# A causal attention layer: VectorE's maximum issued ahead of ScalarE's copy, and inverse roots as exp(-½ ln)

## The chip, the core and the metric

The kernel runs on one core of a Trainium2 chip. A core has five engines with a queue each: TensorE (PE; its weight loads are listed apart as PEld), VectorE (DVE), ScalarE (ACT), GpSimd (POOL) and SyncE (SP, which here starts DMAs). Every engine takes its own instructions strictly in order, and the engines wait for each other by semaphores. The metric is device time in microseconds (us), the median over runs.

## The reference, cut to what matters

Three stages run one after the other on a 64 x 64 image of 256 channels, which is 4096 tokens of 256 values: a windowed linear attention, a causal softmax attention with a small two-layer network behind it, and a mixture of experts. The change lies in the second:

```python
def _layernorm(x, g, b):
    mu = jnp.mean(x, axis=-1, keepdims=True)
    var = jnp.var(x, axis=-1, keepdims=True)
    return (x - mu) * jax.lax.rsqrt(var + LN_EPS) * g + b      # LN_EPS = 1e-5
...
A = jnp.einsum('bqd,bkd->bqk', q, k)
A = jnp.where(causal, A, MASK_FILL) / sqrt(D)
out = jnp.einsum('bqk,bkd->bqd', softmax(A), v) + x
out = _layernorm(out, g_ln, beta_ln)
h = relu(out @ W1.T + b1) @ W2.T + b2
return _layernorm(h, g_lnff, beta_lnff)      # t = t + this; then t is normalised again for the experts
```

So each group of 512 tokens needs three inverse standard deviations per token: one after the attention, one after the small network, and one for the experts' input.

## The kernel before, in words

All products are float32. The causal stage works on pairs `h` of query tiles (256 queries) and pairs `b` of key tiles (256 keys), with `b` from `h` down to 0. A block (h, b) goes through these steps:

- **scores** (L1160): four matmuls (L1170) write 256 keys x 256 queries into one PSUM bank `pa` of which there are two. ScalarE copies the bank to SBUF as `s` (L1182), and VectorE takes the running maximum over key blocks from the same bank (L1186). At b = 0 VectorE folds the maximum (L1189).
- **maxima** (L1192): TensorE turns the folded maximum (L1199), VectorE reduces it over the keys (L1201, L1205), TensorE turns it back (L1212), ScalarE copies it as `tops` (L1214).
- **exponentials** (L1218): VectorE subtracts `tops` from `s` (L1221), ScalarE takes the exponential (L1222).
- **products** (L1228): matmuls with the values accumulate in `po` (L1243); at b = 0 `finish` (L1250) divides, adds the residual and takes mean and variance (L1258 to L1264).

Up to 19 blocks are scored ahead of their exponentials. When four (at the end two, one, one) query tiles of a group are finished, `layers` (L1271) puts a list of small steps on a line; the main loop takes one step from a line when it is due, in between the scores and products:

- `root(mvs)` (L1278, ScalarE: square root of the variance plus eps), `first` (reciprocal on VectorE, L1281, then the scaling, L1287), `turn` (transposes L1295, ScalarE's `aT` L1296), two times `hidden` (L1304, L1306), `last` for each tile (L1313, L1315 and statistics);
- `root(mvy)`, then `scale` for each tile (L1281 again, L1323, L1324, statistics);
- `root(mine)`, then `norm` (L1281, L1332), and `turn_again` (L1349 and ScalarE's L1353), whose result is the experts' input.

There are ten such lines, so thirty roots. After the last block the rest of the lines is emptied one step after another; then the experts' routing starts, with a softmax (`every` L1342, product L1520, exponential L1493, one-hot columns L1572, L1577) from which the weights to load are found.

The order on TensorE, VectorE and ScalarE is the order in which the program emits (a hand-written schedule); GpSimd's and the DMA queues' follow from a scheduler. Two engines that read the same PSUM bank are put one after the other by semaphores: in the kernel before, the maximum waits for the copy, and the matmuls that take the bank again wait for the maximum. [...]

## Time and profile before

| | |
|---|---|
| time, median of 3 runs (lowest, highest) | 1732.9 us (1732.24, 1734.23) |
| time of the profiled execution | 1732.45 us |
| its span, from the first to the last instruction | 1730.8 us |
| causal stage, from L1027's first products to the experts' L1577 | about 825 to 1501 us |
| PE busy / DVE busy / ACT busy / POOL busy | 96% / 58% / 46% / 31% of the span |
| mean granted TensorE clock | 0.985 |
| ACT table loads at L1222 and at L1278 | 21 and 21, 1283 ns each |

The profile is one execution. A group line reads: source line, engine, operation, output tile <- input tiles, shapes, count, then busy time and the mean of one, then the idle time of that engine just ahead of these instructions, with what ended it. A line of the waits reads: who waited, for whom: us in total, times, the longest. A line of the timeline reads: start, duration, engine, line, operation, tiles, count, and in brackets the idle time ahead of it. PEclk is the TensorE clock that was granted, 1.00 being full speed.

### The profile page before, as it was taken

The page shows a single profiled execution, that of the slowest core. Times are in us where ns is not written, and L with a number is a line of the kernel's source. Part 1 is how long each engine was busy: PE and PEld are TensorE (multiplying, and loading weights), DVE is VectorE, ACT ScalarE, POOL GpSimd, SP SyncE. Part 2 cuts the span into 40 slices and gives each one's busy share as a digit, 9 for nine tenths or more (in the row PEclk, how much of TensorE's full clock was granted, in tenths as well). Part 3 has the DMA queues.
Part 4 walks back from the last instruction along what each step waited for, and adds up shares of the span by engine and source line. Part 5 has one row for each costly group of instructions (what it writes and reads, how often), then busy time and mean ns, then how long its engine had stood idle before and what let it go on. Part 6 is the DMA issues. An engine that isn't in the chain of part 4 may idle for free.

```text
span 1730.8 us, 48947 instructions
## 1 busy us (share of the span) xinstructions
PE 1654.3 (96%) x21131; PEld 1257.4 (73%) x21131; DVE 997.1 (58%) x2101; ACT 793.4 (46%) x1539; POOL 540.8 (31%) x819
## 2 busy tenths in 40 slices
PE   5999999999999999999999999999999998699997
PEld 3666666666766666666778888787787776488996
DVE  6545666566645677676443456555645555655656
ACT  3566444444566445544133344444454444344442
POOL 2485435431381533341300220211112021322322
PEclk9999999999999999999999999999999998799999
DMA  8511312112421312122000000000000000100001
GB/s 251 153 66 64 89 54 69 41 47 64 144 76 52 98 43 55 50 57 77 1 1 1 1 1 0 1 0 1 1 1 1 1 1 1 49 1 25 25 13 37
DMA packets 89768, 74.15 MB, mean 43 GB/s; under 512 B 39568, under 2 KB 73512, under 8 KB 89552
## 3 DMA queue, kind: packets, MB, share of 16 engines
q1 hardware_dynamic: 87136, 63.00, 12.2%
q0 software_dynamic: 1264, 3.84, 0.7%
q10 hardware_dynamic: 1152, 4.19, 0.7%
q8 instruction: 165, 2.70, 0.7%
q14 instruction: 51, 0.42, 0.1%
HBM read 53.18 MB, written 17.83 MB: 41 GB/s over the span
## 4 chain that ended last, share of the span: by engine, by line
PE 41%; DVE 6%; ACT 3%; issue 1%; POOL 0%; ACTq 0%; DVEq 0%; POOLq 0%
PE pa L1170 11%; PE po L1243 11%; PE py L1668 6%; PE rb L1603 4%; PE pm L1099 2%; PE pm L1304 2%; PE cd L1603 1%; PE pm L1313 1%; DVE lnst L863 1%; DVE max L1186 1%; PE pm L1027 1%; ACT s L1182 1%; DVE s L1221 1%; DVE t L1324 1%; PE po L1246 1%
## 5 line engine op out<-in xcount | busy, mean ns | idle before, releaser
L382 ACT ACTIVATE pm<-ps 128x448 f32<-128x448 f32 (+22 forms) x674 | 323.5, 545 | 289.0 <-PE ps L433 156.1
L384 DVE TENSOR_SCALAR pm<-ps 128x448 f32<-128x448 f32 (+13 forms) x406 | 240.6, 621 | 214.0 <-PE ps L433 142.8
L433 PE MATMUL ps<-q,kh 32*128 32x188 f32 (+15 forms) x4224 | 193.9, 330 | 1.9 <-issue 1.7
L1170 PE MATMUL pa<-qT,k 128*128 128x256 f32 (+1 forms) x800 | 185.3, 376 | 0.0
L1186 DVE TENSOR_TENSOR max<-max,pa 128x512 f32<-128x512 f32 x105 | 71.8, 683 | 189.9 <-ACT s L1182 189.8
L1170 PEld LDWEIGHTS pa<-qT,k 128*128 128x128 f32 x800 | 150.6, 191 | 23.8 <-issue 2.7
L1222 ACT ACTIVATE s<-s 128x512 f32<-128x512 f32 x136 | 85.5, 630 | 178.4 <-DVE s L1221 174.7
L466 PE MATMUL ps<-pm,vh 128*32 128x188 f32 (+9 forms) x2688 | 148.2, 336 | 0.0
L433 PEld LDWEIGHTS ps<-q,kh 32*128 32x128 f32 (+1 forms) x4224 | 138.7, 169 | 8.5 <-issue 6.1
L502 POOL TENSOR_TENSOR y<-y,rn 128x512 f32<-128x512 f32 x32 | 40.9, 1278 | 305.5 <-DVE y L501 277.7
L1182 ACT COPY s<-pa 128x512 f32<-128x512 f32 x120 | 69.9, 582 | 115.1 <-PE pa L1170 115.0
L1668 PE MATMUL py<-w,hT 128*128 128x256 f32 x512 | 115.7, 379 | 1.1 <-DVE y L1671 1.1
L466 PEld LDWEIGHTS ps<-pm,vh 128*32 128x32 f32 x2688 | 70.8, 109 | 53.0 <-issue 35.2
L1243 PE MATMUL po<-kh,s 128*128 128x257 f32 x406 | 105.6, 388 | 3.0 <-ACT s L1222 3.0
L1668 PEld LDWEIGHTS py<-w,hT 128*128 128x128 f32 x512 | 97.5, 191 | 14.3 <-DVE y L1671 1.5
L420 PE MATMUL ps<-table,table 32*128 32x256 bf16 (+19 forms) x2752 | 105.5, 251 | 0.2 <-ACT kp L667 0.2
L420 PEld LDWEIGHTS <-table 32*128 32x128 bf16 (+1 forms) x2752 | 40.7, 94 | 85.4 <-issue 83.4
L1221 DVE TENSOR_TENSOR s<-s,tops 128x512 f32<-128x512 f32 x136 | 95.2, 703 | 1.0 <-ACT tops L1214 1.0
L586 PE MATMUL ps<-l0wo,y 128*128 128x256 f32 x384 | 90.7, 387 | 0.0
L1235 POOL TENSOR_SCALAR xn<-t,stats 128x256 f32<-128x256 f32 x32 | 42.0, 1318 | 151.0 <-DVE att L1260 150.6
L1243 PE MATMUL po<-v,s 128*128 128x257 f32 x342 | 87.2, 386 | 1.8 <-ACT s L1222 1.8
L1243 PEld LDWEIGHTS po<-kh,s 128*128 128x128 f32 x406 | 75.9, 194 | 16.4 <-ACT s L1222 4.4
(376 smaller groups left out, 3023.3 us busy)
## 6 DMA issues: line engine op xcount, KB each, us to landing
rn<-rscratch SPq DMA_DIRECT2D x48, 256.0 KB
oscratch<-ov SPq DMA_DIRECT2D x32, 256.0 KB
ov<-oscratch SPq DMA_DIRECT2D x32, 256.0 KB
vq<-vscratch SPq DMA_DIRECT2D x80, 64.0 KB
t<-in_xT SPq DMA_DIRECT2D x16, 256.0 KB
vscratch<-v SPq DMA_DIRECT2D x32, 128.0 KB
vh<-vscratch SPq DMA_DIRECT2D x16, 256.0 KB
out<-y SPq DMA_DIRECT2D x7, 512.0 KB
```

The source lines that it names most:

```text
L382: nc.scalar.activation(dst, src, AF.Relu)
L384: nc.vector.tensor_scalar_max(dst, src, 0.0)
L420: nc.tensor.matmul(got[h][ps, spot].rearrange("p (y x) -> p y x", y=part.r1 - part.r0), lhsT=spread[hs, kind, ks], rhs=bias[hs], start=(i ...
L433: nc.tensor.matmul(got[h][ps, spot].rearrange("p (y x) -> p y x", y=part.r1 - part.r0), lhsT=keys[hs], rhs=q[hs, part.r0 : part.r1, part.c ...
L466: nc.tensor.matmul(out, lhsT=v, rhs=pm[:, h, spot].rearrange("p (y x) -> p y x", y=part.r1 - part.r0), start=fresh, stop=(left[key] == 0), ...
L586: nc.tensor.matmul(pt[:, i * D : (i + 1) * D], lhsT=ys[wi, Y][:, (2 * j + i) * P : (2 * j + i + 1) * P], rhs=wo[:, n, :], start=(n == 0), ...
L1170: nc.tensor.matmul(pp[:, k * 2 * P + at : (k + 1) * 2 * P], lhsT=key, rhs=qT[:, c, q0 + at : q0 + 2 * P], start=(c == 0), stop=(c == DC - 1))
L1182: nc.scalar.copy(s, pp)
L1186: nc.vector.tensor_tensor(u["max"], old, pp, op=ALU.max)
L1221: nc.vector.tensor_tensor(s, s, u["top"].unsqueeze(1).to_broadcast([P, 2, 2 * P]), op=ALU.subtract)
L1243: nc.tensor.matmul(acc, lhsT=u[b][:, (2 * k + j) * P : (2 * k + j + 1) * P], rhs=v[2 * b + k][:, 0 : D + 1], start=(b == h and k == 0), st ...
L1668: nc.tensor.matmul(py, lhsT=hT[:, e, f, j * P : (j + 1) * P], rhs=w2v[:, e, f, :], start=(n == 0), stop=(n == len(order) - 1))
```

## The change

In `scores` the two readers of the bank change places: VectorE's maximum is issued first and waits for the matmuls, ScalarE's copy is issued second and waits for the maximum, and the matmuls that reuse the bank wait for the copy. In `layers` each root becomes two activations on ScalarE, a logarithm with bias eps and an exponential with scale -0.5, so that the inverse root comes from ScalarE; the thirty reciprocals on VectorE go.

```diff
             else:
-                nc.scalar.copy(s, pp)
                 old = u["max"]
                 if b == h - 1:
                     u["max"] = sm.tile([P, 512], F32, name="max", bufs=1)
                 nc.vector.tensor_tensor(u["max"], old, pp, op=ALU.max)
+                nc.scalar.copy(s, pp)
...
             def root(var):
-                nc.scalar.activation(var[:, j0:j1, 1], var[:, j0:j1, 1], AF.Sqrt, bias=eps5)
-
-            def inverse(var):
-                nc.vector.reciprocal(var[:, j0:j1, 1], var[:, j0:j1, 1])
+                nc.scalar.activation(var[:, j0:j1, 1], var[:, j0:j1, 1], AF.Ln, bias=eps5)
+                nc.scalar.activation(var[:, j0:j1, 1], var[:, j0:j1, 1], AF.Exp, scale=-0.5)
 
             def first():
-                inverse(mvs)
...
             def scale(j):
                 mvy = state["mvy"]
-                if j == j0:
-                    inverse(mvy)
...
             def norm():
-                inverse(mine)
```

## The prediction

> **What bounds the kernel now.** I read the page first: which engine is full, and where it is not.

> ```profile
> PE 1654.3 (96%) x21131; PEld 1257.4 (73%) x21131; DVE 997.1 (58%) x2101; ACT 793.4 (46%) x1539; POOL 540.8 (31%) x819
> PE   5999999999999999999999999999999998699997
> ACT  3566444444566445544133344444454444344442
> ```

> TensorE is the bound; only its stops count. The causal stage is slices 20 to 35 (825 to 1501 us), and the only real hole is at its end. So I took the table of stretches and TensorE's waits of the stage's steady part.

> ```profile
> 825.00:1445.00 620.00, 600.99 (x2740) 495.75 (x2741) 321.71 (x725) 260.89 (x457) 108.77 (x186) 0.99 0.00 1
> 1467.00:1490.00 23.00, 16.41 (x77) 12.74 (x75) 19.18 (x61) 9.69 (x32) 2.89 (x4) 0.89 0.00 1
> ...
> PE pm L1199 <- DVE fold L1189: 4.4, 9, 1.7
> PE pm L1304 <- ACT aT L1296: 2.8, 1, 2.8
> PE pm L1212 <- DVE wide L1205: 2.6, 3, 1.9
> PE po L1243 <- ACT s L1222: 2.5, 2, 1.8
> PE pm L1295 <- DVE att L1287: 2.3, 1, 2.3
> PE pm L1349 <- DVE att L1332: 2.0, 1, 2.0
> ```

> The columns of the stretches are the length, then busy time of PE, PEld, DVE, ACT, POOL, then the clock. In 620 us TensorE stops for 19.0 us: all that the steady part can give back, besides clock. In the stage's tail (1467 to 1490) TensorE is no bound; a chain of small steps through VectorE, TensorE and ScalarE runs, and ScalarE is busy for 9.69 of 23 us. The timeline of ScalarE shows why so little:

> ```profile
> 1456.41 0.63 ACT L1222 ACTIVATE s<-s 128x512 f32<-128x512 f32 x1
> 1457.06 1.28 ACT L1278 ACT_TABLE_LOAD   x1
> 1458.36 0.30 ACT L1278 ACTIVATE mvy<-mvy,eps 128x4 f32<-128x4 f32 x1
> 1458.67 1.28 ACT L1222 ACT_TABLE_LOAD   x1
> ...
> 1467.16 1.28 ACT L1278 ACT_TABLE_LOAD   x1
> 1468.46 0.29 ACT L1278 ACTIVATE mvs<-mvs,eps 128x1 f32<-128x1 f32 x1
> ...
> 1489.83 0.29 ACT L1278 ACTIVATE stats<-stats,eps 128x1 f32<-128x1 f32 x1 [1.89 <-DVE stats L864]
> ...
> 1492.69 1.28 ACT L1493 ACT_TABLE_LOAD   x1
> ```

> A root among exponentials costs two loads; but after 1467.16 no exponential comes, and nine square roots (1468.46 to 1489.83) share one load.

> **Loads.** The order of instructions of the built programs can be compared. For the kernel before it has 21 loads at L1278, 21 at L1222 and one at L1493, and the trace has the same numbers, so I trust it for the changed one: a load ahead of each of the 30 logarithms, another ahead of each of the 30 new exponentials, one at L1222, none at the softmax; 61 for 43. Up to 1445 us there are 19 roots, so 39 loads for 37: no change there. The other 16 more fall into the tail.
> [...]

> **The tail.** A new root is load, logarithm, load, exponential. From the rows: 1.28 + 0.02 + 0.30 + 0.01 + 1.28 + 0.02, and the exponential itself, which the trace does not show for 4 columns: between 0.19 (the shortest ScalarE entry, an accumulator read) and 0.30 (the square root with its bias tile). I take 0.20, as it has no bias tile: 3.11 us. Nine of them are 28.0 us. ScalarE's other work from 1467.0 to 1490.1 is 9.69 - 1.28 - 9 x 0.295 = 5.75 us. Together 33.8 us where 23.0 us pass now: ScalarE becomes the bound of the tail, +10.8. It can't run quite without a stop: the last logarithm waits for statistics that VectorE begins only after the copies' column sums are in (L1357, 0.17; then 0.47 + 0.48 + 0.43 + 0.18 with gaps, 1.9 us in all), less the load that runs meanwhile (1.28): +0.6. Before 1467 two roots stand among the last exponentials, where TensorE stops for 2.1, 1.5 and 1.5 us on ScalarE already; each gets two 0.20 us steps longer at most: +0.4. Off go a reciprocal (0.16) and what is not hidden of the softmax's load (0.1). Tail: 10.8 + 0.6 + 0.4 - 0.3 = **+11.5**. Bounds: if only the last line's three roots were on the path, 3 x (3.11 - 0.30 - 0.17) = +8; if half of ScalarE's 13 us of idle time stayed, +17. The row that is nearest is the full queue, so 11.5.

> **The exchange of copy and maximum.** The bank comes free after the same two reads (0.58 and 0.68), and TensorE never waits for a bank (L1170 has no such wait). What changes is who is held.

> VectorE is freed: its maximum waits 237.2 us for the copy now. The fold is ready 0.58 sooner; the nine waits of L1199 (0.55, 0.18, 0.18, 0.99, 0.24, 1.74, 0.18, 0.18, 0.18) lose up to that each: -2.9. The 1.9 at L1212 follows such a fold: -0.6. Where roots' loads stood ahead of a copy, VectorE waited for all of it: the maximum at 1396.80 waits 2.74 for a copy at 1396.20, behind two loads; the scaling L1332 then starts at 1397.61. Without that it starts after the new exponential, 1392.76 + 3.11 = 1395.9: the 2.0 at L1349 loses 1.7. Likewise at 1346: -1.1. At 1210: the scale steps, from 1200.65, move to the second root's end, 1192.2 + 3.1 + 0.6 + 3.1 = 1199.1: -1.5.

> ScalarE is bound: the copy now waits for the maximum, behind whatever VectorE has queued, and exponentials and `aT` are queued behind the copy. Where VectorE is late, TensorE pays:

> ```profile
> 1034.60 0.57 ACT L1182 COPY s<-pa 128x512 f32<-128x512 f32 x1
> 1035.06 1.45 ACT L1296 ACTIVATE aT<-pm,ik 128x512 f32<-128x512 f32 x2
> ...
> 1036.61 0.66 DVE L1186 TENSOR_TENSOR max<-max,pa 128x512 f32<-128x512 f32 x1
> ...
> 1036.87 1.88 PE L1304 MATMUL pm<-aT,ik 128*128 128x512 f32 x4
> ```

> The maximum of this bank stands behind a string of `finish` (1033.94 to 1036.69), perhaps 0.6 sooner than now. So the copy ends at about 1037.3, the halves of `aT` follow by 1038.6, and L1304, ready at 1036.87, stops for about 1.2. The same pattern stands at 1068.05 (copy, then `aT`, with `scale` steps on VectorE): another 1.2. At 1351 L1349 gets about 1.3, since a root's 3.11 at 1343.28 now precedes copy and `aT`. The two waits on exponentials: 0.7 loses 0.5, 1.8 gains 0.3. Sum of the stops: -2.9 - 0.6 - 1.7 - 1.1 - 1.5 + 1.2 + 1.2 + 1.3 - 0.2 = **-4.3**.

> **Clock.** After the stops of 2.79, 2.25 and 2.03 us (at 1211, 1348 and 1399) the clock row is 0.50 for 3.4 us; eight products that take 1.73 elsewhere take up to 3.4: about 1.7 us each. Stops of 1.92, 1.83 and 1.74 were not followed by this. In the changed kernel I expect two such stretches for three: the 1.83 grows to 2.1, and at 1345 to 1351 two stops (1.1 and 1.3) lie close. **-1.7**.
> [...]

> **Free of charge.** The 30 reciprocals (0.17 each) lie on an engine that is idle for half the stage; 19 exponentials in the steady part add 4 us to a ScalarE that is busy for 261 of 620 us. Two GpSimd instruction pairs (L1235 against L1177 and L1179) change order on an idle queue; SyncE's queue is as before. If GpSimd's cover were gone, it would be one 1.3 us step (L1235) each.

> **Sum.** Profiled execution 1732.45, span 1730.8 (the median of the runs, 1732.9, is 0.45 above): 1732.45 + 11.5 - 4.3 - 1.7 = 1738.0 us. About 0.2% (3.5 us) is what a measurement of this kernel can tell from no change.

> **Rivals.**
> *Freed VectorE wins (not slower).* One mechanism: with the 237 us of waits gone, VectorE runs so far ahead that the copies never wait, and the three new stops don't arise. Stops -8.0, all three clock stretches gone -5.1: -13.1; with a tail of +10.8 that gives 1730. It decides once the steady part gains over 12. For it: VectorE is busy for only 52% of the steady part. Against it: the row at 1036.61, where VectorE is late without waiting for anybody.
> *Bound ScalarE loses more.* If the stop of 1.2 comes in each of the seven four-tile lines, the steady part has 8.4 of new stops in place of 2.4, and one or two clock stretches more than I count: +3 in place of -6; with the tail 1747. Against it: in most lines there is more slack than at 1036.
> *The change does not do what the order shows.* If no table load stood between logarithm and exponential, all loads of the stage would go: the 5.1 us of stops at 1452 to 1461, the load at 1467, and the stops and clock of the steady part (-9 with clock), tail +0: about 1718. Against it: the order, whose counts the trace confirms.

> **How the numbers follow.** Forecast 0.60 (own range 1734 to 1743, from a tail of 10 to 14 and a steady part of -8 to -3.5), freed VectorE 0.20, bound ScalarE 0.18, no loads 0.02. Faster than 1729.4: a third of freed VectorE and no loads, 0.08. Within 0.2%: the rest of freed VectorE (0.14) and the forecast's low end (0.10). Slower: 0.68. The range leaves out the fast end of the second case and the slow end of the third: 1729 to 1747.

> **What would show it.** In the profile after: 30 loads each at the two root lines, 1283 ns; ScalarE all but full from 1467 for about 34 us; L1520 some 12 us further behind the last L1243 than now; maxima waiting for PE, copies for DVE; L1199's waits below 2 us in all; new stops at L1304 behind `aT`. If TensorE's stops up to the last score shrink by over 8 us, or the tail grows by less than 8, the forecast is wrong there.

## The result and the profile after

The changed kernel takes **1737.66 us** in the median of 11 runs (1735.58 to 1741.43), the kernel before 1732.36 (11 runs, 1728.87 to 1734.33, the three of the table above among them). The ratio is 1.0032, with a 95% interval from 1.0022 to 1.0043: slower by 5.3 us, or 0.3%. The profiled execution took 1737.66 too, with a span of 1735.9.

The page of the changed kernel, the lines that answer to those shown of the kernel before:

```profile
PE 1652.6 (95%) x21131; PEld 1256.1 (72%) x21131; DVE 995.7 (57%) x2071; ACT 819.9 (47%) x1587; POOL 541.7 (31%) x819
PE   5999999999999999999999999999999997599997
ACT  3567444444566444544133345445454456544442
```

TensorE's busy time is no longer than before; the hole near slice 34 is deeper, and ScalarE is fuller there. VectorE has the 30 reciprocals less, ScalarE 30 steps and 18 loads more. TensorE's waits in the steady part of the causal stage (825 to 1441 us):

```profile
PE pm L1301 <- ACT aT L1293: 2.5, 3, 1.1
PE po L1243 <- ACT s L1222: 2.5, 2, 2.2
PE pm L1212 <- DVE wide L1205: 1.8, 3, 1.1
PE pm L1343 <- ACT aT L1293: 1.6, 1, 1.6
PE pm L1199 <- DVE fold L1189: 1.4, 2, 1.0
PE pm L1292 <- DVE att L1284: 1.0, 1, 1.0
```

The list has changed sides. The waits for VectorE (`fold`, `wide`, `att`) have shrunk, and nearly half of what is left, 6.6 us on the lines shown, is for ScalarE: for exponentials (2.5 us, as before) and for `aT`, which now stands behind copies that wait for maxima. With the small lines that are not shown the sum is 13.7 us, for 19.0 before. Between the two readers it went as forecast: over the whole program the maximum waits 199.1 us for TensorE and the copy 212.7 us for the maximum, where the maximum waited 237.2 us for the copy.

The tail in ScalarE's timeline (start, duration, instruction, idle time ahead of it):

```profile
1464.24 0.81 ACT L1293 ACTIVATE aT<-pm,ik 128x128 f32<-128x128 f32 x2 [2.64 <-PE pm L1292]
1465.06 1.28 ACT L1278 ACT_TABLE_LOAD   x1
1466.36 0.30 ACT L1278 ACTIVATE stats<-stats,eps 128x4 f32<-128x4 f32 x1
1466.67 1.28 ACT L1279 ACT_TABLE_LOAD   x1
1467.97 0.21 ACT L1279 ACTIVATE stats<-stats 128x4 f32<-128x4 f32 x1
...
1477.31 0.81 ACT L1293 ACTIVATE aT<-pm,ik 128x128 f32<-128x128 f32 x2 [1.22 <-PE pm L1292]
...
1494.46 0.29 ACT L1278 ACTIVATE stats<-stats,eps 128x1 f32<-128x1 f32 x1 [0.53 <-DVE stats L864]
1496.07 0.20 ACT L1279 ACTIVATE stats<-stats 128x1 f32<-128x1 f32 x1
```

Load, logarithm, load, exponential, and the next load at 1468.19: from 1464.24 the queue is full but for short stops, with loads as its bulk: 16 of 1283 ns up to the last root's end at 1496.27, 20.5 of 32.0 us. TensorE waits:

```profile
1443.91 1.14 PE L1243 MATMUL po<-vh,s 128*128 128x257 f32 x4 [2.05 <-ACT s L1222]
...
1496.77 1.01 PE L1334 MATMUL pm<-ik,att 128*128 128x1 f32 x4 [6.59 <-DVE att L1326]
...
1506.86 2.02 PE L1571 MATMUL py<-byexpert,b 8*128 8x2 f32 x8 [0.64 <-DVE byexpert L1568]
```

The first and the last of these lines are the marks by which I compare all kernels. In the kernel before they are:

```profile
1452.94 1.14 PE L1243 MATMUL po<-vh,s 128*128 128x257 f32 x4 [2.11 <-ACT s L1222]
...
1501.08 2.02 PE L1577 MATMUL py<-byexpert,b 8*128 8x2 f32 x8 [0.64 <-DVE byexpert L1574]
```

The first is TensorE's stop on the last pair's exponentials: the end of the steady part. The last is the end of the routing, after which the expert stage runs. Their distance is the tail: 62.95 us, for 48.14. The steady part runs from the stage's first matmul at L1099 (846.59 us, before 846.80) to the first mark. It is 8.8 us shorter, the tail 14.8 longer.

### The profile page after: what moved, and what is told of

It reads as the page before. It is cut to its first block, busy times and chain, and to the rows that moved or that the text cites. A ratio compares the mean times of both kernels' runs of the same rounds, so it can differ in the third digit from the quotient of the medians.

```text
span 1735.9 us, 48897 instructions
## 1 busy us (share of the span) xinstructions
PE 1652.6 (95%) x21131; PEld 1256.1 (72%) x21131; DVE 995.7 (57%) x2071; ACT 819.9 (47%) x1587; POOL 541.7 (31%) x819
## 4 chain that ended last, share of the span: by engine, by line
PE 40%; DVE 5%; ACT 5%; issue 1%; POOL 0%; DVEq 0%; ACTq 0%; POOLq 0%
PE pa L1170 11%; PE po L1243 10%; PE py L1662 6%; PE rb L1597 4%; PE pm L1099 2%; PE cd L1597 1%; PE pm L1301 1%; PE pm L1310 1%; ACT L1279 1%; ACT L1278 1%; DVE lnst L863 1%; PE pm L1027 1%; PE po L1246 1%; DVE t L1319 1%; DVE max L1185 1%
## 5 line engine op out<-in xcount | busy, mean ns | idle before, releaser
L1170 PE MATMUL pa<-qT,k 128*128 128x256 f32 (+1 forms) x800 | 184.5, 375 | 0.0
L1186 ACT COPY s<-pa 128x512 f32<-128x512 f32 x120 | 70.1, 584 | 212.7 <-DVE max L1185 212.7
L1170 PEld LDWEIGHTS pa<-qT,k 128*128 128x128 f32 x800 | 149.6, 190 | 23.3 <-issue 2.2
L1222 ACT ACTIVATE s<-s 128x512 f32<-128x512 f32 x136 | 85.3, 629 | 70.8 <-DVE s L1221 70.4
L1243 PE MATMUL po<-kh,s 128*128 128x257 f32 x406 | 105.6, 388 | 3.0 <-ACT s L1222 3.0
L1235 POOL TENSOR_SCALAR xn<-t,stats 128x256 f32<-128x256 f32 x32 | 43.5, 1366 | 157.8 <-DVE att L1260 157.4
L1243 PEld LDWEIGHTS po<-kh,s 128*128 128x128 f32 x406 | 75.8, 194 | 16.4 <-ACT s L1222 4.4
L1243 PE MATMUL po<-v,s 128*128 128x257 f32 x342 | 85.5, 380 | 2.2 <-ACT s L1222 2.2
```

The source lines that it names most:

```text
L1170: nc.tensor.matmul(pp[:, k * 2 * P + at : (k + 1) * 2 * P], lhsT=key, rhs=qT[:, c, q0 + at : q0 + 2 * P], start=(c == 0), stop=(c == DC - 1))
L1243: nc.tensor.matmul(acc, lhsT=u[b][:, (2 * k + j) * P : (2 * k + j + 1) * P], rhs=v[2 * b + k][:, 0 : D + 1], start=(b == h and k == 0), st ...
```

## The experiments

Six kernels, beside the two, by these marks; "stops" are TensorE's recorded stops within the steady part, without the one at the mark, "half clock" its stretches of 3.4 us at half clock (6.8 counts as two). The median is over all runs of a kernel, the other columns are of its one profiled execution. What lies behind the last mark took 229.0 to 232.1 us in these executions, so steady part and tail don't add up to the differences of the medians.

| kernel | median us | loads in the stage | steady us | stops us | half clock | tail us |
|---|---|---|---|---|---|---|
| before | 1732.4 | 43 | 606.1 | 18.3 | 3 | 48.1 |
| changed | 1737.7 | 61 | 597.3 | 13.0 | 1 | 62.9 |
| exchange alone | 1720.9 | 43 | 593.0 | 10.3 | 1 | 48.9 |
| roots alone | 1757.6 | 61 | 616.1 | 22.4 | 6 | 63.1 |
| changed, one shared load | 1708.3 | 1 | 586.3 | 7.2 | 0 | 40.5 |
| changed, square roots in the tail | 1722.9 | 45 | 595.6 | 13.0 | 0 | 48.0 |
| one shared load, copy first | 1714.2 | 1 | 594.6 | 10.5 | 1 | 42.1 |
| changed, aT and hT by VectorE in the tail | 1736.1 | 61 | 599.0 | 13.0 | 2 | 58.8 |

**The exchange alone.** Kernel before, with

```diff
-                nc.scalar.copy(s, pp)
...
                 nc.vector.tensor_tensor(u["max"], old, pp, op=ALU.max)
+                nc.scalar.copy(s, pp)
```

> The kernel before with the exchange of maximum and copy alone; square root and reciprocal stay. Theory (the two parts add: the exchange earns the 9.0 us by which the first stop on an exponential at the end comes earlier, 1452.94 to 1443.91, and the roots' loads cost the 14.8 us by which the tail is longer): TensorE's stops before that point shrink by 4 to 8 us, at least one half-clock stretch of 3.4 us goes, the tail stays at 48 us; 1732.4 - 7 to 9 = about 1724. Rival A (the steady part was eased by the 30 reciprocals taken off VectorE, not by the exchange): 1731 to 1733. Rival B (a bound ScalarE makes new stops in the steady part, which the new roots' timing only happened to hide): above 1733.

1720.91 us (6 runs; ratio 0.994, interval 0.9925 to 0.9955): 11.1 us faster, more than I expected. The steady part is 13.1 shorter, the tail 0.7 longer. So the exchange eases the steady part by itself, and both rivals fall.

**The roots alone.** Changed kernel, with the copy ahead of the maximum again.

> The changed kernel with the copy ahead of the maximum again: the logarithm and exponential alone, 60 loads. Theory: tail longer by 14 to 16 us as in the changed kernel; in the steady part VectorE's maximum now waits for copies behind four-step roots (3.1 us in place of 1.6), so its stops grow by 0 to 5 us; 1732.4 + 14 to 20 = 1746 to 1752. Rival A (the steady gain belongs to the roots): about 1738, as the changed kernel. Rival B (the tail's growth needs the exchange as well, copies held behind maxima): tail near 48 us and 1733.

1757.6 us (4 runs; ratio 1.0143, interval 1.0127 to 1.0159): 25.6 us slower, more than I expected. The tail is as in the changed kernel, as the theory has it; both rivals fall. But the steady part is 10 us longer than before, where I had put 0 to 5. The parts don't add: -11.1 and +25.6 would make +14.5, and together they make +5.3. The timeline of this kernel shows what the exchange has to do with the roots:

```profile
1353.74 1.28 ACT L1279 ACT_TABLE_LOAD   x1
1355.04 0.21 ACT L1279 ACTIVATE stats<-stats 128x4 f32<-128x4 f32 x1
1355.15 0.57 ACT L1182 COPY s<-pa 128x512 f32<-128x512 f32 x1
1355.75 0.69 DVE L1186 TENSOR_TENSOR max<-max,pa 128x512 f32<-128x512 f32 x1 [4.30 <-ACT s L1182]
1356.82 2.30 PE L1292 MATMUL pm<-ident,att 128*128 128x128 f32 x8 [3.56 <-DVE att L1284]
```

The copy stands behind a whole root, 3.1 us; the maximum waits 4.30 us for the copy; VectorE's scaling (L1284) stands behind the maximum, and TensorE waits 3.56 us for it. In the changed kernel the same stop is 0.99. Stops and half clock account for most of the 10 us: 4.1 us more stops, and three stretches more at 1.7 each.

**One shared load.** Changed kernel, and at the stage's start:

```diff
+            nc.scalar.preload_act_table_set("natural_log_exp_and_others")
```

> The changed kernel with one load, asked for by name at the stage's start, of a table that holds both logarithm and exponential; one line more, nothing else. Theory (the 60 loads are the cost): no load between the stage's start and the experts, a root takes 0.30 + 0.21 us in place of 3.1, ScalarE's stretch in the tail falls from 38 to some 15 us of work and the tail is bound by TensorE again at 43 to 48 us, less than the 48.1 of the kernel before, since its last root's load (1.28) and the stops behind the two loads among the last exponentials go as well; steady part as in the changed kernel or 1 to 3 us better; 1716 to 1722. Rival A (not the loads but the longer chain of two dependent activations, with a wait between, holds the tail): above 1731. Rival B (the table placed by name is loaded over by the compiler's own loads): 60 loads still there, 1738.

1708.3 us (4 runs; ratio 0.9864, interval 0.9846 to 0.9883): the fastest of all, 23.7 us below the kernel before and 29 below the changed one. Its groups hold one load for the 60:

```profile
L1279 ACT ACTIVATE stats<-stats 128x4 f32<-128x4 f32 (+2 forms) x10 | 2.1, 206 | 0.3
...
L1429 ACT ACT_TABLE_LOAD x1 | 1.3, 1283 | 0.0
```

Both rivals fall. The same two activations in a chain, without loads, make a tail of 40.5 us, shorter than the square roots' 48.1; its last root shows how little the hop costs:

```profile
1461.90 0.29 ACT L1278 ACTIVATE stats<-stats,eps 128x1 f32<-128x1 f32 x1 [1.83 <-DVE stats L864]
1462.23 0.20 ACT L1279 ACTIVATE stats<-stats 128x1 f32<-128x1 f32 x1
1462.47 0.41 DVE L1326 TENSOR_SCALAR att<-t,stats 128x256 f32<-128x256 f32 x1 [0.60 <-ACT stats L1279]
1462.94 1.01 PE L1334 MATMUL pm<-ik,att 128*128 128x1 f32 x4 [3.42 <-DVE att L1326]
```

The wait at L1334 is 3.42, where the changed kernel has 6.59. So it is the loads, not the logarithm and exponential, that made this change slower. The steady part gained more than I gave it: 11.0 us against the changed kernel, of which the stops are 5.8 and the half-clock stretch 1.7; the other 3.5 have no line of their own. With the set asked for by name the trace has one load for the 60 steps; without that, it has a load at each of the 60, of 1283 ns. What a root would cost on VectorE (adding eps, then the power -0.5) stays open: the kernel written for it has no time.

**Square roots in the tail.** Changed kernel; the eleven roots issued once the last pair's products have begun are square root and reciprocal again.

```diff
             def root(var):
+                if emptying:
+                    nc.scalar.activation(var[:, j0:j1, 1], var[:, j0:j1, 1], AF.Sqrt, bias=eps5)
+                    state["square"] = True
+                    return
...
+            def inverse(var):
+                if state.pop("square", False):
+                    nc.vector.reciprocal(var[:, j0:j1, 1], var[:, j0:j1, 1])
```

> The changed kernel in which the roots of the tail alone (those issued once the last pair's products have begun) are square root and reciprocal again; the exchange and the new roots stay in the steady part. Theory: steady part as in the changed kernel (first stop on an exponential at the end near 1443.9), tail as in the kernel before (48 us, one or two us more, since the last new root's tables have to be left): 1723 to 1726. Rival A (the tail is longer because ScalarE arrives in it with more work left over from the steady part, so its own roots matter little): above 1732. Rival B (half of each): 1728 to 1731.

1722.93 us (5 runs; ratio 0.9953, interval 0.9939 to 0.9966), tail 48.0: at the low end of what was expected. Rival A and Rival B fall; the tail's growth is all in the tail's own roots.

**One shared load, copy first.** The kernel with one load, with the exchange undone.

> The kernel with one shared load, with the copy ahead of the maximum again. What the exchange is worth without loads: it was worth 11.1 us with square roots (two loads and 0.3 a root) and 19.9 with logarithm and exponential (two loads and two steps, and nothing hidden). Theory (the exchange earns by letting VectorE pass the loads that stand ahead of a copy on ScalarE): without loads only the fold's 0.58 and the shorter aT queue remain, 2 to 5 us: 1710 to 1713. Rival (it earns by the order of the two reads of a bank itself, whatever stands in the queue): 10 us or more, 1718 or above.

1714.2 us (4 runs; ratio 0.9891, interval 0.9872 to 0.991), 5.9 us above the kernel with the exchange, which has four runs too. The runs of each spread over nearly 6 us, and relative to the kernel before beside them the difference is 4.7 us (0.9891 less 0.9864), so the theory's 2 to 5 can't be told from a little more; the rival's 1718 lies above all four runs. The exchange is worth about 5 or 6, 11 and 20 us with no load, with the square roots' loads, and with logarithm and exponential apart; in the steady part of the profiled executions it is 8.3, 13.1 and 18.8. So its value grows with what stands in ScalarE's queue ahead of a copy, but it is not all loads: some of it comes without any.

**Relief of ScalarE in the tail.** Changed kernel; `aT` and `hT` by VectorE once the last pair's products have begun.

```diff
             def hidden(e):
...
+                if emptying:
+                    nc.vector.tensor_scalar(state["hT"][:, e, 0:width], pp[:, 0:width], col["b1"][:, e : e + 1], 0.0,
+                                            op0=ALU.add, op1=ALU.max)
+                    return
```

and likewise for `aT` in `turn`.

> The changed kernel, its 60 loads kept, with ScalarE's steps aT and hT of the tail (those issued once the last pair's products have begun) made by VectorE instead. It tells why the tail of the changed kernel is 62.9 us and not the 59.6 of the forecast. From the first load of the tail to the last root's end ScalarE takes 38.1 us there: 28.0 of roots, about 5.6 of aT, hT and column sums, and 4.5 idle, waiting for transposes. Theory (the idle time comes from ScalarE and TensorE waiting for each other in turn: hT stands behind a root's loads, TensorE stops for hT in front of the transposes that ScalarE waits for next): with aT and hT off ScalarE both go, 4.7 us of steps and most of the 4.5 idle, down to the roots and column sums: tail 54 to 57 us, 1730 to 1732 (as against 1737.7). Rival A (ScalarE is simply full, the idle time is there for another reason): only the 4.7 us of steps, tail 58 to 59, 1733 to 1734. Rival B (the chain of statistics, root, scaling sets the tail, not ScalarE's queue): tail 62 to 63, 1737 to 1738.

1736.08 us (12 runs; ratio 1.0011, interval 1.0001 to 1.0022; the kernel before took 1733.47 beside it). Beside the kernel before that is 2.6 us slower, where the changed kernel is 5.3; the profiled execution had one half-clock stretch more in the steady part than that of the changed kernel, and took 2.4 us longer behind the last mark. So the time is above the 1733 to 1734 of Rival A, but the tail is 58.8 us, 4.2 shorter: Rival A's number for it, the moved steps and no more. ScalarE still idles in the tail, now for statistics:

```profile
1467.34 0.30 ACT L1278 ACTIVATE stats<-stats,eps 128x4 f32<-128x4 f32 x1 [3.69 <-DVE stats L864]
```

From 1467.34 to the last root its queue is full but for 0.53 (at 1492.12, again for statistics) and the gaps between instructions. So ScalarE is the bound of the tail's later part, and my theory, that the idle time goes with `aT` and `hT`, falls. Why the work arrives late has another answer in this kernel than in the changed one. Here VectorE, which makes the statistics, is itself full with the moved steps: it has no recorded stop from 1462.75 to 1473.83. In the changed kernel the 2.64 us ahead of 1464.24 are TensorE's: the rows to be turned are ready at 1461.69, but eight of the last pair's products (L1243, 1462.19, 1.90 us) stand ahead of the transposes, which start at 1463.93.

## Why the prediction was right

The forecast, 1738.0, and the sign came out, by the mechanism that was forecast: a shorter steady part, and a longer tail with ScalarE as its bound. That the number is met to 0.3 us is luck. The tail was 3.3 us dearer than its term, stops and clock together 2.7 us cheaper than theirs, and the runs of the changed kernel alone spread over 5.9 us. By the prediction's own steps:

- **Loads.** 30 and 30 at the root lines, 1283 ns each, one at L1222, none at the softmax: as forecast. The exponential takes 206 ns for the 0.20 estimated, a root in the tail 3.1 us for 3.11.
- **Tail, +11.5: measured +14.8.** The step that was mis-sized is "can't run quite without a stop: +0.6". From the first root load behind the last exponential (1458.13) to the last root's end (1496.27) are 38.1 us, where 23.0 passed before. Ahead of that load nothing was lost for the +0.4 forecast, behind the last root 0.4 was gained for 0.3. Work is 33.6 of them, for 33.8 forecast; idle time is 4.5 (2.64, 1.22, 0.53 and 0.15). I had let the full queue begin at the tail's first load, but it begins at 1464.24, 6 us later: until then ScalarE waits for transposes that stand behind TensorE's products. The 1.22 us, at 1477.31, hold something that the forecast had no term for, TensorE's clock in the tail, which is 0.73 over these 38.1 us: four products ahead of those transposes (L1310, 1474.98) take 2.07 us at half clock, 1.03 elsewhere. The tail is the same with the exchange and without it (62.9 and 63.1), and 48.0 with square roots in it, so its growth belongs to its own roots.
- **Exchange, stops -4.3: measured -5.3.** Single stops came out close: L1199 lost 3.0 (2.9 forecast), the one at 1396 lost 1.6 (1.7), that at 1346 lost 1.3 (1.1), that at 1210 lost 1.7 (1.5), L1349's new stop behind `aT` is 1.56 (1.3). The two new stops at L1304 (now L1301) are where they were expected, but of 0.88 and 0.55 for 1.2 each: VectorE was less late than I took it to be.
- **Clock, -1.7: measured about -3.4.** One stretch for three, where I had left two. The price of 1.7 us a stretch was right: the changed kernel and the one with square roots in the tail have the same 13.0 us of stops, one stretch and none, and differ by 1.7 in the steady part; the kernel with VectorE's `aT` has two, the same stops, and is 1.7 longer again. Their number goes, in these traces, with where the stops fall on a grid of 3.413 us that the forecast did not know of (below), so that two were expected and one came speaks neither for the forecast nor against it.
- **"Free of charge": 19 exponentials in the steady part.** Not free by themselves: with the copy first the new roots cost 10.0 us there. Beside the exchange they cost 4.3 (597.3 for 593.0). The stops of the forecast were worked out with both parts in place, and so its sum didn't suffer; its sentence on the exponentials counted only ScalarE's busy time, not those who wait behind it.
- **Rivals.** "Freed VectorE wins" put stops of -8.0 and three stretches at -13.1 in the steady part. The exchange alone has the same sums (stops -8.0, steady part -13.1), but one stretch is left there, so 1.7 us of the 13.1 are neither stops nor clock, and that they agree is chance. Beside the new roots the steady part gains 8.8, and the tail was dearer. "Bound ScalarE loses more" did not come: three new stops behind `aT`, as forecast, not seven. "No loads between logarithm and exponential" was no case for this kernel, but the kernel in which it is true runs at 1708, 10 us below the 1718 given to it: its steady part is 19.8 us shorter than before, where 9 was given, and its tail 7.6, where stops of 5.1 and one load were given.

## What to carry to other kernels

Count the table loads of the built program before counting activations: here the same two functions took 1737.7 us with 61 loads in the stage and 1708.3 with one, when one table for both was asked for by name. Where two engines read the same buffer, try both orders. Here VectorE first was better in all three pairs of kernels (1720.9 for 1732.4 us, 1737.7 for 1757.6, 1708.3 for 1714.2), though VectorE is the busier of the two in the steady part (322 us against 261), and what it brought depended on what was queued ahead of ScalarE's copy. So measure the order of readers and the work in the queue together and not as separate terms. And where a queue becomes the bound, ask from which moment its work has arrived, not only how much it is.

## What the runs showed of the hardware

The same stop of TensorE is at one time followed by half clock and at another not. In the changed kernel and in that with square roots in the tail the stop of 2.23 us ahead of L1243 is one and the same; here the 3.4 us that hold it and the 3.4 us after them in the changed kernel (length, busy time of PE with its instructions, of PEld, DVE, ACT and POOL, then the clock):

```profile
902.20:905.61 3.41, 1.18 (x7) 0.88 (x6) 2.50 (x5) 2.95 (x5) 0.00 (x0) 1.00 0.00 0
905.61:909.02 3.41, 3.41 (x6) 1.34 (x5) 0.00 (x0) 1.06 (x3) 0.77 (x2) 0.50 0.00 0
```

and, of the kernel with square roots in the tail, the 3.4 us that begin 1 us after the stop:

```profile
904.00:907.40 3.40, 3.40 (x12) 2.07 (x11) 0.00 (x0) 1.75 (x4) 0.77 (x2) 1.00 0.00 0
```

In the second line half as many matmuls run as in the third. In the kernels with one shared load a stop of 2.04 us at 1432.50 passed at full clock, and one of 2.05 at 1441.00 (copy first) was followed by half clock. So the forecast's reading of its three stretches, by which a stop grown to 2.1 us is followed by half clock, was too sharp: it can be.
